# Layer 3 of a spectral network: where two pieces of statistics stand in the VectorE queue

## The chip, the cores and the metric

The kernel runs on one core of a Trainium2 chip. The metric is the device time of one execution in microseconds, lower is better; the time shown for a kernel is the median of its timed executions. Engines are called by the names of the profile: PE is TensorE (PEld its weight loads), DVE is VectorE, ACT is ScalarE, POOL is GpSimd, and SP is SyncE, which here only issues DMAs.

## The reference

Eight images of 8 channels and 256x256 pixels pass through two layers with residuals. The first normalizes x over groups and runs a small Fourier neural operator on it: a lift to 40 channels, four rounds of a spectral convolution (12x12 low and high modes) plus a grouped 1x1 convolution, with a gated activation after the first three, and then two 1x1 convolutions with 512 channels between them. The second normalizes again and takes a 3x3 maximum.

```python
def ref(xg):                                   # _L0_conv_ref, x normalized in groups
    h = gconv1x1(concat(xg, grid), fc0_w, fc0_b)
    for i in range(4):
        h1 = spectral_conv(h, sp_w1[i], sp_w2[i])
        h2 = gconv1x1(h, w_w[i], w_b[i])
        h = h1 + h2
        if i < 3:
            h = gswish(h, betas[i])
    h = gswish(gconv1x1(h, fc1_w, fc1_b), betas[3])
    return gconv1x1(h, fc2_w, fc2_b)
x = x + ref(gn(x))
x = x + dilate3x3(gn(x))
```

`gn` needs mean and variance of x over each of four groups of two channels, for each image. Everything is in float32.

## The kernel before

The images run one after the other, and the work of an image is laid over that of its neighbours. For image b, `layers` runs the four layers (`l` from 0 to 3). Each has a short spectral part (`spectrum_h`, `mix`: modes by weights, on DVE mostly), then the rows of the inverse transform (`rows_even` or `rows_odd`: matmuls into PSUM banks `p_g`, copied into the SBUF tile `zt`), and then `layer`: 11 chunks of pixels, for each a `burst(c)` of matmuls into `p_z`, first the 1x1 convolution (L590), then the columns of the inverse transform out of `zt` (L593), and an ACT instruction that writes h back (L598, or L600 in layer 3, after which L602 stores the chunk to DRAM).

Three other strands are woven in. The head of the image before (fc1, activation, fc2 and the sum into y) is cut into steps: `first` is four matmuls into `p_fc` (L813) and two ACT activations (L814, L815); `second` is fc2 (L830), whose sum DVE adds to y (L839). The tail of the image before is the dilation, on DVE (L877 to L893). The third strand is `side`, the generator `start(b + 1)`: the statistics and spectrum of the next image's x (`spectrum_x`). It advances by one piece for each `next(side, None)`. Its first two pieces are the two passes of the loop at L268: four `bn_stats` (L271) each, one per group, on one half of x in `turned`. What comes after is `bn_aggr` (L275), the sums over partitions on PE (L260, L262), the reciprocal root, the normalization (L296), and the transforms. For the last image there is no next one, and `side` yields nothing.

The order of instructions on PE, DVE, ACT and SP is the order in which the Python code emits them (`tc.manual_schedule`); semaphores are put in from the tiles that are read and written. The generators yield short strings that name what to weave in at that point: "f" is a `first`, "c" a `second`, "t" a piece of the tail. Image 0 has no head before it, so nothing is woven into its layers (`alone[0]`).

The lines that the change touches are in `rows_odd`, which serves layers 1 and 3. It makes the rows in two groups: (0..5) and (6..9). Each takes four PSUM banks, one from the ring "one" and three from the ring "tri", both of two buffers, which `p_fc` and `p_z` share. The matmuls of a group are at L509. `copy_banks` shares its copies out (L215 on ACT, L217 on DVE); in the second group ACT has copies 1, 4 and 5 and DVE has 0, 2 and 3. In layer 3 a piece of `side` is taken after each group: after the first group's copies and the head's steps "fc", and after the second group's copies and "f". `hold(last)` then ties loads that were held back behind the last row matmul.

The image 0..7 of this text is b of the code. The first burst of layer 3 needs the `zt` copies of both groups for L593, and a free `tri` buffer for L590.

Of the kernel before, what the change touches and what calls it, by code (L numbers as in the profile page):

```python
# [46 lines left out]
def fno_dilate_kernel(ctx: ExitStack, tc: tile.TileContext, a: dict, out: bass.AP):  # L47
# [17 lines left out]
    def ps_four(name):  # L65
        one, tri = ps_a(f"{name}_0"), ps_tri(f"{name}_1")
        return one, tri, [one] + [tri[:, i, :] for i in range(3)]

    def part(i):
        return slice(32 * i, 32 * i + 32)  # L70
# [139 lines left out]
    def copy_banks(pairs, by_act):  # L210

        done = []
        for i, (dst, src) in enumerate(pairs):
            if i in by_act:
                ins = nc.scalar.activation(dst, src, AF.Identity).ins  # L215
            else:
                ins = nc.vector.tensor_copy(dst, src).ins  # L217
            for other in done:
                if other.engine != ins.engine:
                    tc.declare_no_dep(ins, other, reason="two engines read banks of one tile and write apart")  # L220
            done.append(ins)
# [274 lines left out]
    def rows_odd(b, l, side):  # L496

        zv = zt[:, :, :, : NBLK * WID].rearrange("p r g (n o) -> p g o n r", n=NBLK)
        hold()
        yield "ffc"  # L500
        for part_of, by_act, kinds in ((((0, 1, 2), (3, 4, 5)), (2, 3), "fc"), (((9,), (6, 7, 8)), (1, 4, 5), "f")):
            one, tri, banks = ps_four(f"p_g_{b}_{l}_{part_of[0][0]}")
            pairs = []
            for i, os in enumerate(part_of):
                for at, o in enumerate(os):
                    for j in range(NQ):
                        for k in range(2):
                            two = slice(64 * k, 64 * k + 64)
                            last = mm(banks[2 * i + k][part(j), 2 * NBLK * CS * at : 2 * NBLK * CS * (at + 1)],  # L509
                                      fz2[two, o, :], rowg[two, j].rearrange("p g x -> p (g x)"),  # L510
                                      start=True, stop=True)
                for k in range(2):
                    src = banks[2 * i + k][:, : 2 * NBLK * CS * len(os)]
                    src = src.rearrange("p (o g n r) -> p g o n r", g=2, n=NBLK, r=CS)
                    dst = zv[:, 2 * k : 2 * k + 2, os[0] : os[-1] + 1]
                    if len(os) == 1:
                        pairs.append((dst[:, :, 0], src[:, :, 0]))
                    else:
                        pairs += [(dst[:, g], src[:, g]) for g in range(2)]
            copy_banks(pairs, by_act)  # L520
            yield kinds
            if l == 3:
                next(side, None)
        hold(last)
        if l < 3:
            yield "t"
# [164 lines left out]
    def layers(b, stored, d, then, ahead):  # L691

        for l in range(4):
            if l > 0:
                yield from spectrum_h(b, l, d)
                yield from mix(b, l, d)
            yield from rows_odd(b, l, then) if l % 2 else rows_even(b, l)  # L700
            yield from layer(b, l, d, stored, then, ahead)
        yield "stored"
        yield from rest(b, then)
# [60 lines left out]
    def hold(after=None):  # L764

        due, held[0] = held[0], [] if after is None else None
        for f in due or ():
            tc.add_manual_dep(f().ins, after.ins.name, BEHIND, reason="load behind the rows")
# [355 lines left out]
```

## Time and profile before

| what | value |
|---|---|
| three timed runs | 3701.52, 3705.54, 3706.05 us |
| median | 3705.54 us |
| profiled execution | 3705.41 us |
| its span, first to last instruction | 3703.6 us |
| mean granted PE clock | 0.977 |
| PE busy | 3495.7 us (94%) |
| ACT busy | 2864.6 us (77%) |
| DVE busy | 2385.4 us (64%) |
| `bn_stats` on x (L271) | 64 instructions, median 678 ns |
| `zt` copies on DVE (L217) | 266 instructions, median 533 ns |

The span is the time between the first and the last instruction of the profiled execution; the execution's own time is 1.8 us longer. Busy PE is not PE at its peak: matmuls are pipelined, and the ends of their records are modelled. Rows of the timeline give the start in us from the span's beginning, the length in us, engine, line, operation, output and inputs, shape, how many are merged into the row, and in brackets the idle time of the engine just before with what ended it. The releaser is inferred: of several that a wait asks for, the one that came last by the profile. The chain of waits goes back from the last instruction to what released it, step by step. In the table of windows the granted clock of PE stands after the five engines, as a share of full speed.

### The profile page before, as it was taken

The page shows a single profiled execution, that of the slowest core. Times are in us where ns is not written, and L with a number is a line of the kernel's source. Part 1 is how long each engine was busy: PE and PEld are TensorE (multiplying, and loading weights), DVE is VectorE, ACT ScalarE, POOL GpSimd, SP SyncE. Part 2 cuts the span into 40 slices and gives each one's busy share as a digit, 9 for nine tenths or more (in the row PEclk, how much of TensorE's full clock was granted, in tenths as well). Part 3 has the DMA queues.
Part 4 walks back from the last instruction along what each step waited for, and adds up shares of the span by engine and source line. Part 5 has one row for each costly group of instructions (what it writes and reads, how often), then busy time and mean ns, then how long its engine had stood idle before and what let it go on. Part 6 is the DMA issues. An engine that isn't in the chain of part 4 may idle for free.

```text
span 3703.6 us, 112658 instructions
## 1 busy us (share of the span) xinstructions
PE 3495.7 (94%) x50872; PEld 1271.0 (34%) x50872; DVE 2385.4 (64%) x3711; ACT 2864.6 (77%) x3021; POOL 117.1 (3%) x202
## 2 busy tenths in 40 slices
PE   5768999999999999999999999999999999999997
PEld 2323333333333333333333333333333333333222
DVE  6776666557775677746776577765777567772443
ACT  2435888888788888787887878888888878879986
POOL 1000000000000000000000000000000000000000
PEclk7878999999999999999999999999999999999998
DMA  3005111432225212261223512244222522225221
GB/s 91 16 19 205 52 50 46 160 110 72 72 83 190 81 55 66 92 220 52 60 62 125 181 55 74 65 159 122 64 75 89 183 76 61 72 64 194 82 83 48
DMA packets 114081, 344.71 MB, mean 93 GB/s; under 512 B 15985, under 2 KB 18481, under 8 KB 98177
## 3 DMA queue, kind: packets, MB, share of 16 engines
q1 hardware_dynamic: 95392, 276.32, 24.6%
q0 software_dynamic: 18208, 61.18, 5.0%
q8 instruction: 400, 6.55, 0.7%
q14 instruction: 81, 0.66, 0.1%
HBM read 213.44 MB, written 123.74 MB: 91 GB/s over the span
## 4 chain that ended last, share of the span: by engine, by line
PE 73%; DVE 16%; issue 4%; ACT 4%; DMA 2%; POOL 0%; ACTq 0%; DVEq 0%; POOLq 0%
PE p_fc L830 20%; PE p_fc L813 19%; PE p_z L593 9%; PE p_z L590 7%; PE p_d L558 7%; PE p_z L587 3%; DVE y L839 3%; PE p_u L572 3%; DVE turned L541 3%; DVE S L414 3%; DVE turned L411 2%; DMA yin<-y_rows 2%; PE p_b L381 1%; ACT act L815 1%; ACT act L814 1%
## 5 line engine op out<-in xcount | busy, mean ns | idle before, releaser
L815 ACT ACTIVATE act<-p_fc 128x1536 f32<-128x1536 f32 x1024 | 1493.1, 1458 | 0.0
L813 PE MATMUL p_fc<-hs,c_w 32*128 32x512 f32 x8192 | 1133.2, 625 | 40.2 <-DVE y L839 20.8
L830 PE MATMUL p_fc<-act,c_w 128*32 128x512 f32 x8192 | 1008.6, 601 | 0.2 <-ACT act L815 0.2
L814 ACT ACTIVATE act<-p_fc 128x512 f32<-128x512 f32 x1024 | 616.5, 602 | 229.7 <-PE p_fc L813 218.2
L541 DVE STREAM_TRANSPOSE turned<-h 128x1024 f32<-128x1024 f32 x528 | 632.7, 1226 | 189.7 <-ACT h L598 189.2
L598 ACT ACTIVATE h<-p_z 128x512 f32<-128x512 f32 (+1 forms) x528 | 511.9, 1021 | 212.2 <-PE p_z L593 212.2
L839 DVE TENSOR_TENSOR y<-p_fc,y 128x512 f32<-128x512 f32 x392 | 267.7, 683 | 553.9 <-PE p_fc L830 553.9
L813 PEld LDWEIGHTS p_fc<-hs,c_w 32*128 32x128 f32 x8192 | 357.7, 183 | 612.8 <-ACT act L814 253.3
L830 PEld LDWEIGHTS p_fc<-act,c_w 128*32 128x32 f32 x8192 | 221.8, 109 | 705.0 <-issue 330.7
L593 PE MATMUL p_z<-c_binv,zt 32*128 32x256 f32 x5632 | 411.7, 406 | 2.1 <-DVE zt L217 2.1
L590 PE MATMUL p_z<-h,c_wt 32*32 32x512 f32 x8448 | 363.5, 606 | 15.7 <-DVE zt L217 7.7
L593 PEld LDWEIGHTS p_z<-c_binv,zt 32*128 32x128 f32 x5632 | 259.8, 187 | 312.4 <-issue 300.0
L558 PE MATMUL p_d<-turned,c_fw 32*32 32x480 f32 (+1 forms) x9216 | 307.8, 539 | 0.6 <-DVE turned L541 0.2
L600 ACT ACTIVATE h<-p_z,c_bias 128x512 f32<-128x512 f32 (+1 forms) x176 | 186.4, 1110 | 89.1 <-PE p_z L593 89.0
L562 ACT ACTIVATE turned<-p_d 128x1440 f32<-128x1440 f32 x144 | 182.9, 1270 | 89.7 <-PE p_d L558 86.5
L215 ACT ACTIVATE zt<-p_g 128x198 f32<-128x198 f32 (+2 forms) x118 | 53.4, 575 | 182.8 <-PE p_g L487 99.9
L414 DVE TENSOR_REDUCE S<-turned 128x80 f32<-128x800 f32 x192 | 189.0, 984 | 5.9
L411 DVE TENSOR_TENSOR turned<-t,B 128x800 f32<-128x800 f32 x192 | 188.7, 983 | 0.9
L558 PEld LDWEIGHTS p_d<-turned,c_fw 32*32 32x32 f32 x9216 | 127.0, 103 | 165.8 <-issue 64.9
L372 DVE STREAM_TRANSPOSE turned<-zt 128x960 f32<-128x960 f32 x96 | 176.8, 1865 | 2.5
L590 PEld LDWEIGHTS p_z<-h,c_wt 32*32 32x32 f32 x8448 | 93.2, 103 | 186.8 <-DVE y L839 48.8
L572 PE MATMUL p_u<-turned,c_stack 128*32 128x480 f32 (+1 forms) x1152 | 136.7, 543 | 11.6 <-DVE turned L561 6.2
(192 smaller groups left out, 1762.8 us busy)
## 6 DMA issues: line engine op xcount, KB each, us to landing
stored<-h SPq DMA_DIRECT2D x88, 1024.0 KB
hs<-stored SPq DMA_DIRECT2D x352, 256.0 KB
t<-in_spw SPq DMA_DIRECT2D x96, 400.0 KB
yin<-y_rows POOLq DMA_DIRECT2D x56, 512.0 KB, 5.2
h<-in_xp SPq DMA_DIRECT2D x352, 48.0 KB
turned<-in_xw SPq DMA_DIRECT2D x16, 1024.0 KB
y<-in_x SPq DMA_DIRECT2D x56, 256.0 KB
y_rows<-y POOLq DMA_DIRECT2D x56, 256.0 KB, 3.9
```

What stands on the lines that cost most here:

```text
L411: nc.vector.tensor_tensor(pr, sw[k], bt[:, k2, k].unsqueeze(2).to_broadcast([128, G, 2 * WID, WID]), ALU.mult)
L414: nc.vector.tensor_reduce(s[k2][:, k].rearrange("p s o g -> p (s o) g"), pr.rearrange("p g m i -> p m g i"), AX.X, ALU.add,)
L541: nc.vector.transpose(dst[:, 2 * i : 2 * i + 2], h[:, c, 2 * i : 2 * i + 2].rearrange("p f (s x) -> p f s x", s=2))
L558: mm(banks[q][part(v % 4), : 240 * n], fw8[part(q), v, :], t[part(q), :, :, v, : NBLK * WID], start=v < 4, stop=v >= 4)
L590: mm(o, wt[part(q), l, g, :], h[part(q), c, f, :], start=True, stop=False)
L593: mm(banks[q][:, HW * s : HW * (s + 1)], zt[part(q), 2 * c + s].rearrange("p f o -> p (f o)"), binv[part(q), :], start=False, stop=s == 1)
L598: nc.scalar.activation(dst, src, AF.Silu)
L813: mm(banks[g], w1[part(g), blk, :], hs[k][part(g), :], start=True, stop=True)
L814: nc.scalar.activation(act[:, 0, :], one, AF.Silu)
L815: nc.scalar.activation(act[:, 1:4, :], tri, AF.Silu)
L830: mm(acc[part(g), :], w2[:, g, 15 - rb - i : 47 - rb - i], act[:, g, :], start=i == 0, stop=i == 1)
L839: nc.vector.tensor_tensor(y, sums, y, ALU.add)
```

## The change

In layer 3, `next(side, None)` is no longer called in the loop over the two row groups; it is called twice behind the loop, still ahead of `hold(last)`.

```diff
             copy_banks(pairs, by_act)
             yield kinds
-            if l == 3:
-                next(side, None)
+        for _ in range(2 if l == 3 else 0):
+            next(side, None)
         hold(last)
         if l < 3:
             yield "t"
```

On DVE, in images 0 to 6, the order was: copies of the first group, (addition L839), four `bn_stats`, three copies of the second group, four `bn_stats`. It becomes: copies of the first group, (addition L839), three copies of the second group, eight `bn_stats`. The addition is there in images 1 to 6. The orders on the other engines stay as they are, and so does what each instruction waits for. Layer 1, which runs the same function, doesn't change.

## The prediction

> **What bounds the kernel now.** I read the page first, then the chain of waits in the stretches where layer 3 begins, then the timeline of all engines in those stretches, and last the table of windows with the granted clock. From the page, the shares of the chain that ended last by engine:
>
> ```profile
> PE 73%; DVE 16%; issue 4%; ACT 4%; DMA 2%; POOL 0%; ACTq 0%; DVEq 0%; POOLq 0%
> ```
>
> So the end is set by TensorE (PE) for most of the span and by VectorE (DVE) for a sixth of it; a piece of DVE work that stands on the chain is worth its length. The statistics (L271) are such a piece. Chain of waits around the start of layer 3 of image 1 (start, us, what):
>
> ```profile
> 689.03 0.69 DVE y L839
> ...
> 690.24 1.86 DVE bn_x L271 x3
> 692.10 0.30 DVE zt L217
> ...
> 692.45 1.92 PE p_z L590 x32
> ```
>
> The chain leaves PE at 689.0, goes through an addition, through four `bn_stats`, through the first copy into `zt`, and comes back to PE at 692.45. The statistics belong to the next image, and nothing near here needs them: they are on the chain because DVE takes its queue in order and the copies stand behind them. The timeline of the same place, all engines:
>
> ```profile
> 689.64 2.46 DVE L271 BATCH_NORM_STATS2 bn_x<-turned 128x6 f32<-128x512 f32 x4
> 690.03 1.14 PE L813 MATMUL p_fc<-hs,c_w 32*128 32x512 f32 x8
> 690.13 1.09 ACT L215 ACTIVATE zt<-p_g 128x132 f32<-128x132 f32 x3 [1.01 <-PE p_g L509]
> 691.74 1.45 ACT L815 ACTIVATE act<-p_fc 128x1536 f32<-128x1536 f32 x1
> 692.02 1.06 DVE L217 COPY zt<-p_g 128x132 f32<-128x132 f32 x3
> 693.19 0.27 PEld L590 LDWEIGHTS p_z<-h,c_wt 32*32 32x32 f32 x30 [0.62 <-ACT act L815]
> 694.30 1.15 PE L593 MATMUL p_z<-c_binv,zt 32*128 32x256 f32 x16
> 695.46 2.12 ACT L600 ACTIVATE h<-p_z,c_bias 128x512 f32<-128x512 f32 x2 [2.28 <-PE p_z L593]
> ```
>
> ACT copies its three banks of the second row group at 690.13, as soon as PE has made them; DVE copies its three only at 692.02. PE ends `p_fc` at 691.17 and stands until 692.45, makes two pieces of L590, and stands again to 693.19, the end of the last DVE copy (692.02+1.06 = 693.08) plus 0.11. The row names ACT L815 for that second stop because it too ends at 693.19; but L815 reads the other `tri` buffer. `p_z` takes the buffer of `p_g`, two takings back in a ring of two, and waits for the `zt` copies. ACT then stands 2.28 us before L600. Both engines have run dry, and the work that would fill them waits for three copies.
>
> The kernel holds its own counter-sample. Image 7 has no next image, so no statistics stand there. The same stretch of image 7:
>
> ```profile
> 3332.28 1.36 DVE L217 COPY zt<-p_g 128x132 f32<-128x132 f32 x3
> 3332.67 1.14 PE L813 MATMUL p_fc<-hs,c_w 32*128 32x512 f32 x8
> 3332.77 1.11 ACT L215 ACTIVATE zt<-p_g 128x132 f32<-128x132 f32 x3 [1.01 <-PE p_g L509]
> 3333.74 1.35 PE L590 MATMUL p_z<-h,c_wt 32*32 32x512 f32 x32
> 3335.01 1.15 PE L593 MATMUL p_z<-c_binv,zt 32*128 32x256 f32 x16
> ```
>
> From the start of L813 to the start of L593 it is 2.34 us here, against 694.30-690.03 = 4.27 in image 1.
>
> [...] the bank was there by 690.13 (ACT took its share then) and DVE came 1.89 us later. [...] The trace shows such half-rate windows right behind this stall in images 0, 3 and 4; the windows of image 3, with busy times of PE, PEld, DVE, ACT, POOL, then the granted clock:
>
> ```profile
> 1568.30:1571.60 3.30, 2.02 (x26) 0.52 (x20) 3.30 (x8) 3.03 (x5) 0.00 (x0) 0.99 0.45 128
> 1571.70:1575.00 3.30, 3.30 (x47) 1.42 (x45) 1.99 (x4) 0.00 (x0) 0.00 (x0) 0.51 0.08 28
> ```
>
> PE was busy 2.02 of 3.30 us in the stretch with the stall, and the next ran at 0.51. Images 1, 2, 5 and 6 had the same stall and no such window[...]. [...]
>
> **The change part by part.** It removes and adds no instruction. On DVE, in images 0 to 6, four `bn_stats` (2.46 us) go from ahead of the three copies of the second row group to behind them, next to the other four. PE, ACT, POOL and SP keep their order, and every instruction waits for the same producers as before; no DMA moves in any queue. The two halves of x which the statistics read have landed already (DVE shows no idle time before them), and they are read later than now.
>
> *Images 1 to 6.* DVE ends the addition at 689.72 and turns to the copies; they end as in image 7, 3333.64-3331.53 = 2.11 us after the row matmuls (L509) began, so at 688.89+2.11 = 691.00 instead of 693.08. PE is busy with L813 to 691.17, ACT copies to 691.22: what is late next is those, not DVE. By image 7 the gain to L593 is 4.27-2.34 = 1.93 us per image; by the waits, 694.30 less (691.22+0.14+1.08, the L590 block after its last bank is free) = 1.86. I take 1.93, since it is measured with the copies of both engines side by side, and keep 1.86. Six images: 11.6 us. In the other five the row L590 shows 1.27 or 1.28 us of idle time, like image 1, so one number serves for all.
>
> Does it last? ACT, 2.28 us idle before L600, would be 0.35 us idle, as in image 7. From L593 of burst 0 to L590 of burst 1 it is 4.89 us in image 1 and 4.90 in image 7: the lead isn't lost on the way. Loads and stores are issued by these same instructions and move with them.
>
> *What stands behind the statistics now.* The eight in a row end about 690.9+4.85 = 695.75 (now 695.36). Behind them is the addition L839, whose matmul now ends at 698.15, then at 696.22: 0.5 us of room. The aggregation (L275) comes after that addition, and PE asks for it at 705.43. Cost: nothing, covered by that 0.5 us; if the cover were gone, each us more delays the bank that the next burst takes.
>
> *Image 0.* Nothing is interleaved here, and the path is another one:
>
> ```profile
> 296.70 2.42 DVE L271 BATCH_NORM_STATS2 bn_x<-turned 128x6 f32<-128x512 f32 x4
> 299.03 1.04 DVE L217 COPY zt<-p_g 128x132 f32<-128x132 f32 x3
> 300.22 1.15 PE L593 MATMUL p_z<-c_binv,zt 32*128 32x256 f32 x16 [2.10 <-DVE zt L217]
> 304.94 0.49 PE L260 MATMUL p_st_x<-mv_x,avg 128*128 128x4 f32 x2
> ```
>
> The copies would end at 296.70+1.04 = 297.74 and L593 follow L590 at once, at 298.05: 2.17 us earlier. But then L260 needs the statistics, which end when they do now, plus the same 0.14 or so: the aggregation at 302.85, L260 at 302.97 instead of 304.94. PE arrives at 301.4 and waits 1.6 us. So image 0 gains 304.94-302.97 = 1.97, and the releaser changes from the copies to the statistics. The bounds: 0.4 us, if that new wait trips a half-rate window (priced below at 1.55), and 2.17, if the statistics come sooner than thought. I take 1.97.
>
> *Half-rate windows.* In image 3, L590 takes 2.79 us against 1.92 in image 1 and L593 1.83 against 1.15: 0.87+0.68 = 1.55 us; image 4 is alike (2.79 and 1.89). With the stall gone PE is idle for a few tenths in such a stretch, and I take both windows as gone: 3.1 us (image 0's lies where PE will wait anyhow, and counts nothing). Bounds: nothing, if windows fall elsewhere instead (four more lie in other parts of the span), and some 5 us, if one or two of those go too.
>
> *Sum.* 11.6+1.97+3.1 = 16.7 us. The profiled execution took 3705.41 us, 3703.6 of them in the span; 3705.41-16.7 = 3688.7. The median of the runs shown, 3705.54, lies 0.1 above this execution, so it stands for them. I forecast 3689.
>
> **The rivals.**
> 1. The stall goes, the windows do not: the two of images 3 and 4 land elsewhere and image 0 makes one. 3705.4-11.6-0.4 = 3693.4. For it: [...] the runs before spread over 4.5 us. Against it: three of the seven stalls were followed by one at once, none after image 7's start without a stall.
> 2. ACT is the pace of layer 3, and a lead beyond its idle time is lost. Before L600 of burst 1 ACT is idle for only 0.47 us; if just that is kept, 6×0.47+2.0 = 4.8, so 3700.6. Against it: image 7, where the lead lasts into burst 1.
> 3. The change doesn't do what it says: L590 waits for ACT L815, as the row of 693.19 has it. Then only image 0 gains, 3703.4. Against it: image 7's L590 begins at 3333.74, before its L815 (3334.38); and in image 0 a row without an L815 has the same 0.11 us after a DVE copy.
> 4. Slower: the block of eight holds up the addition L839, its bank and so burst 1, and in image 0 the aggregation. It decides once the block ends more than 0.5+1.93 = 2.4 us later than worked out, that is at 0.92 us a piece instead of 0.61. At 1.0 us a piece: 3.1-2.43 = 0.7 lost in each of six images, and 1.1 in image 0: some 5 us, 3710.5. Against it: both groups of four run at 0.61 now, one beside matmuls and the other beside ACT.
>
> **How the numbers follow.** The forecast as it stands 0.62, rival 1 0.23, rival 2 0.07, rival 3 0.04, rival 4 0.04. The likeliest gives 3689. The range reaches from 3685 (gone windows elsewhere too) to 3697 (rival 1 with one or two windows more), which leaves rivals 2 to 4 out. Within 0.2% (7.4 us, about what a measurement can tell from no change) lie rivals 2 and 3; faster by more is anything below 3698.1: 0.86; same 0.10; slower 0.04.
>
> **What would show it.** Right: L271 is gone from the chain in images 1 to 6; L813 to L593 takes about 2.3 us in each; ACT is idle some 0.35 us before the first L600; L839 still waits for PE behind the block; in image 0, L260 waits for the aggregation; no half-rate window right behind the start of layer 3. Wrong: L590 still waiting at its old distance, L839 starting late behind L271, or a longer idle time later in layer 3 that takes the lead back.

## The result, and the profile after

| | before | changed |
|---|---|---|
| median of 6 timed runs | 3703.75 us (3700.28 to 3706.05) | 3689.73 us (3682.43 to 3695.7) |
| profiled execution | 3705.41 us | 3688.73 us |
| its span | 3703.6 us | 3687.0 us |

The ratio is 0.9962, with a 95% interval from 0.9951 to 0.9973. The two profiled executions lie 16.7 us apart, the medians 14.0.

The chain of waits at the start of layer 3 of image 1, in the changed kernel (start, length, what):

```profile
686.40 1.13 PE p_g L509 x63
687.53 1.07 PE p_fc L813 x8
688.60 1.27 PE p_z L590 x32
689.88 1.08 PE p_z L593 x16
```

Addition, statistics and copy are gone from it; PE goes from one block to the next. The timeline of all engines there:

```profile
687.07 1.36 DVE L217 COPY zt<-p_g 128x132 f32<-128x132 f32 x3
687.46 1.14 PE L813 MATMUL p_fc<-hs,c_w 32*128 32x512 f32 x8
687.57 1.11 ACT L215 ACTIVATE zt<-p_g 128x132 f32<-128x132 f32 x3 [1.01 <-PE p_g L509]
688.28 4.80 DVE L271 BATCH_NORM_STATS2 bn_x<-turned 128x6 f32<-128x512 f32 x8
688.53 1.35 PE L590 MATMUL p_z<-h,c_wt 32*32 32x512 f32 x32
689.81 1.15 PE L593 MATMUL p_z<-c_binv,zt 32*128 32x256 f32 x16
690.97 2.12 ACT L600 ACTIVATE h<-p_z,c_bias 128x512 f32<-128x512 f32 x2 [0.35 <-PE p_z L593]
693.73 0.69 DVE L839 TENSOR_TENSOR y<-p_fc,y 128x512 f32<-128x512 f32 x1 [0.65 <-PE p_fc L830]
```

From L813 to L593 it is 2.35 us, as it was in image 7 before; L590 has no idle time left in its row, ACT stands 0.35 us before L600 instead of 2.28, and the eight statistics run under all of this. The addition behind them still finds DVE idle, by 0.65 us.

In image 0 the chain passes through the statistics in another way:

```profile
295.96 1.63 DVE zt L217 x5
297.60 4.64 DVE bn_x L271 x8
302.24 0.34 DVE mv_x L275 x4
...
302.71 0.36 PE p_st_x L260 x2
```

The copies are done early, L593 starts at 297.86, and PE runs on until L260, which asks for the aggregation. The block of eight is the bound there now.

To see where the time went, each ACT instruction of the one profile can be set against the same instruction of the other, since their order is the same. The lead is the start in before less the start in the changed kernel, as the median over a dozen instructions on each side of a step; "between" is what happened from there to the next image.

```
start of layer 3    lead in -> out    gained   between
image 0             0.25 ->  2.60      2.35     -0.03
image 1             2.57 ->  4.49      1.92     +0.51
image 2             5.00 ->  6.83      1.83     -4.05   two half-rate windows more
image 3             2.78 ->  6.18      3.40     +3.18   two fewer
image 4             9.36 -> 13.01      3.65     +0.03
image 5            13.04 -> 14.96      1.92     -1.55   one more
image 6            13.41 -> 15.26      1.85     +1.42   one fewer
```

The seven starts give 16.9 us, and the last instruction leads by 16.7. What lies between adds up to -0.5 us, but only because half-rate windows came and went in equal number. By this table a window counts for 1.4 to 2.0 us.

### The profile page after: what moved, and what is told of

Read it like the earlier page. It is cut to its first block, busy times and chain, and to the rows that moved or that the text cites. A ratio compares the mean times of both kernels' runs of the same rounds, so it can differ in the third digit from the quotient of the medians.

```text
span 3687.0 us, 112658 instructions
## 1 busy us (share of the span) xinstructions
PE 3486.2 (95%) x50872; PEld 1270.1 (34%) x50872; DVE 2386.8 (65%) x3711; ACT 2865.0 (78%) x3021; POOL 117.1 (3%) x202
## 4 chain that ended last, share of the span: by engine, by line
PE 73%; DVE 16%; issue 5%; ACT 4%; DMA 2%; POOL 0%; ACTq 0%; DVEq 0%; POOLq 0%
PE p_fc L830 20%; PE p_fc L813 19%; PE p_z L593 9%; PE p_d L558 7%; PE p_z L590 7%; PE p_z L587 3%; DVE y L839 3%; PE p_u L572 3%; DVE turned L541 3%; DVE S L414 3%; DVE turned L411 2%; DMA yin<-y_rows 2%; DVE turned L372 1%; PE p_b L381 1%; PE p_g L509 1%
## 5 line engine op out<-in xcount | busy, mean ns | idle before, releaser
L815 ACT ACTIVATE act<-p_fc 128x1536 f32<-128x1536 f32 x1024 | 1493.2, 1458 | 0.0
L813 PE MATMUL p_fc<-hs,c_w 32*128 32x512 f32 x8192 | 1133.4, 625 | 41.2 <-DVE y L839 20.8
L839 DVE TENSOR_TENSOR y<-p_fc,y 128x512 f32<-128x512 f32 x392 | 267.9, 684 | 539.1 <-PE p_fc L830 539.1
L813 PEld LDWEIGHTS p_fc<-hs,c_w 32*128 32x128 f32 x8192 | 358.3, 183 | 613.4 <-ACT act L814 253.3
L593 PE MATMUL p_z<-c_binv,zt 32*128 32x256 f32 x5632 | 410.3, 405 | 0.0
L590 PE MATMUL p_z<-h,c_wt 32*32 32x512 f32 x8448 | 357.8, 601 | 7.9 <-ACT act L814 4.2
L593 PEld LDWEIGHTS p_z<-c_binv,zt 32*128 32x128 f32 x5632 | 258.9, 186 | 308.0 <-issue 295.1
L600 ACT ACTIVATE h<-p_z,c_bias 128x512 f32<-128x512 f32 (+1 forms) x176 | 186.4, 1110 | 72.0 <-PE p_z L593 71.8
L590 PEld LDWEIGHTS p_z<-h,c_wt 32*32 32x32 f32 x8448 | 92.9, 103 | 175.3 <-DVE y L839 48.8
```

Source lines behind the costliest of these rows:

```text
L590: mm(o, wt[part(q), l, g, :], h[part(q), c, f, :], start=True, stop=False)
L593: mm(banks[q][:, HW * s : HW * (s + 1)], zt[part(q), 2 * c + s].rearrange("p f o -> p (f o)"), binv[part(q), :], start=False, stop=s == 1)
L813: mm(banks[g], w1[part(g), blk, :], hs[k][part(g), :], start=True, stop=True)
L815: nc.scalar.activation(act[:, 1:4, :], tri, AF.Silu)
L839: nc.vector.tensor_tensor(y, sums, y, ALU.add)
```

## The experiments

The half-rate windows of PE after the first layers, from the clock record of each trace (start in us; 3.4 us long, or 6.8 where two follow each other, marked with x2; the granted clock in them is 0.50 in before and in the changed kernel). The stretch of 24 to 25 us at half rate at the very end, which every trace has, is left out. The kernels in the list are explained below.

```
before            302, 1572, 1653, 1677, 2015, 2974, 3548
changed           1206, 1230, 2544, 3531
changed, again    359, 1209, 1233, 1650, 2111 x2, 3537
image0_only       1648, 2089, 2969, 3543
images1to6_only   301, 772, 2523, 3533
both_ahead        301 x2, 700, 1140 x2, 1584 x2, 2028 x2, 2471 x2, 2915 x2, 3571
four_more_behind  794 x2, 1214, 1583, 2023, 2559, 2999
one_more_behind   768, 2519, 2959, 3533
image0_in_gap     1643, 2521, 3531
```

**Image 0 alone, and images 1 to 6 alone.** Two kernels make the change for one part of the images each.

```diff
-            if l == 3:
+            if l == 3 and not alone[0]:
                 next(side, None)
+        for _ in range(2 if l == 3 and alone[0] else 0):
+            next(side, None)
         hold(last)
```

> The statistics go behind the copies in image 0 only. Theory (each image pays its own stall, and a lead once won is kept): in the profile the layer-3 start of image 0 gains about 2.3 us over before (L260 released by the aggregation, near 302.7 us), and images 1 to 6 keep 4.27 us from the start of L813 to the start of L593. The time moves by 2.3 us at most, plus or minus some half-rate windows of 1.6 us. Rival (image 0's lead is swallowed by the DMA-heavy stretch behind it, 310 to 340 us): the lead is back to zero at 400 us.

One execution took 3700.88 us. The lead over before goes from 1.6 us ahead of the start of image 0 to 4.0 behind it, so 2.4 are won there, and it stands at 3.8 us at 545 us: the stretch full of DMAs (their share is 1.00 to 1.02 from 310 to 340 us in before) doesn't take it. Images 1 to 6 keep 4.27 us from L813 to L593. The same new wait is seen as in the changed kernel:

```profile
301.32 0.35 PE L260 MATMUL p_st_x<-mv_x,avg 128*128 128x4 f32 x2 [1.52 <-DVE mv_x L275]
```

The absolute place, 302.7, wasn't reached because this execution was 1.6 us ahead before anything had changed.

The other half has `not alone[0]` and `alone[0]` exchanged.

> The statistics go behind the copies in images 1 to 6 only; image 0 as before. Theory: 6 times 1.9 = 11.4 us less than before from the stalls, plus what half-rate windows behind them cost before (0 to 3 us): some 3690 to 3692 against a before of 3703.75. L813 to L593 is about 2.35 us in images 1 to 6, and image 0 keeps its half-rate window near 302 us. Rival (most of the gain was image 0 and luck with the half-rate windows): 3698 or more.

3690.61 us, ratio 0.9958 (0.9943 to 0.9973). The distance is 2.35 or 2.36 us in all six images, and image 0 keeps its window, at 301. The gain is images 1 to 6 for the most part.

**Both pieces ahead of the copies.** The stall is made longer, to see whether the price follows the length and whether the half-rate windows follow the stall.

```diff
-            if l == 3:
+            for _ in range(2 if l == 3 and part_of[0][0] == 0 else 0):
                 next(side, None)
```

> Both pieces stand ahead of the second group's copies, so that eight bn_stats precede them. Theory: each of the seven stalls grows by 2.44 us, so 6 times 2.44 = 14.6 us more than before in images 1 to 6 and up to 2.4 in image 0; [...] a half-rate window follows nearly every stall (5 more at 1.5 us, 7.5): 3718 to 3728 against 3703.75. L813 to L593 is 6.7 us or more. Rival A (ACT sets the pace of layer 3 and takes up a delay of PE): under 3712. Rival B (half-rate windows fall by chance and not behind stalls): 3718 to 3721 and no more such windows at the seven places than in the profile of before.

3728.31 us, ratio 1.0063 (1.0048 to 1.0078). That is 0.3 us above the upper end of what the theory gave (3718 to 3728), and past both rivals. TensorE in image 3, as a timeline and then in three windows (busy PE, PEld, DVE, ACT, POOL, then the granted clock):

```profile
1579.88 1.14 PE L813 MATMUL p_fc<-hs,c_w 32*128 32x512 f32 x8
1581.75 1.04 PE L590 MATMUL p_z<-h,c_wt 32*32 32x512 f32 x2 [0.73 <-ACT act L814]
1585.42 2.02 PE L590 MATMUL p_z<-h,c_wt 32*32 32x512 f32 x30 [2.63 <-DVE zt L217]
1587.37 2.09 PE L593 MATMUL p_z<-c_binv,zt 32*128 32x256 f32 x16
```

```profile
1581.00:1584.20 3.20, 1.06 (x6) 0.13 (x2) 3.20 (x6) 2.01 (x3) 0.00 (x0) 0.97 0.53 161
1584.30:1587.60 3.30, 2.18 (x34) 0.54 (x38) 0.98 (x4) 0.00 (x0) 0.00 (x0) 0.50 0.00 0
1587.70:1591.00 3.30, 3.30 (x26) 1.60 (x22) 0.00 (x0) 1.52 (x2) 0.00 (x0) 0.53 0.00 0
```

From L813 to L593 it is now 7.49 us in images 2 to 6 and 6.65 in image 1. Behind the stop, 30 pieces of L590 take 2.02 us (all 32 took 1.35 in image 7 of before), and L593 takes 2.09 instead of 1.15. That nearly every stall would be followed by a half-rate window was an estimate; all seven starts are followed by one, six of them by two (in image 3 the two rows above at 0.50 and 0.53). Here the second stop of L590 has the right name: the wait for the copy ends long after ACT L815.

**More work behind the eight.** Rival 4 rested on the room that the addition L839 has. In images 1 to 6, further `bn_stats`, whose result is not used, follow the eight: one or four.

```diff
         for _ in range(2 if l == 3 else 0):
             next(side, None)
+        if l == 3 and not alone[0] and b + 1 < n_img:
+            more = sb.tile([128, 6], F32, tag="bn_more", bufs=1, name=f"bn_more{b}")
+            for i in range(4):
+                nc.vector.bn_stats(more, turned[:, 1, 512 * i : 512 * i + 512])
         hold(last)
```

> As the change, with one more bn_stats (0.61 us) in images 1 to 6 behind the eight; its result is not used. Theory (the block has 0.65 us of room before the addition L839 is asked for): no cost or a tenth of a us per image. From L593 of burst 0 to L590 of burst 1 it stays at 4.89 us, and the time is that of the changed kernel within its spread, 3686 to 3693. Rival (every us behind the copies costs, room or not): 6 times 0.6 = 3.6 us more, and 5.3 us or more between those two points.

3689.69 us, ratio 0.9957 (0.994 to 0.9973). DVE in image 1 (the addition is L843 here, since lines moved by four):

```profile
686.21 1.36 DVE L217 COPY zt<-p_g 128x132 f32<-128x132 f32 x3
687.41 4.80 DVE L271 BATCH_NORM_STATS2 bn_x<-turned 128x6 f32<-128x512 f32 x8
692.14 0.67 DVE L527 BATCH_NORM_STATS2 bn_more<-turned 128x6 f32<-128x512 f32 x1
692.87 0.69 DVE L843 TENSOR_TENSOR y<-p_fc,y 128x512 f32<-128x512 f32 x1
```

The addition comes 7.27 us after the one before it, as in the changed kernel (693.73 against 686.46), and bursts 0 and 1 stay 4.89 us apart in all six images. The room is used up and nothing is lost.

> As the change, with four more bn_stats in images 1 to 6 behind the eight; their result is not used. Theory (the addition L839 stands behind the block with about 0.6 us of room, and PE needs its bank almost at once): the block ends 2.4 to 2.8 us later, the addition comes 1.8 to 2.2 us late, and burst 1 starts 1.6 to 2.1 us late in each of six images: 10 to 13 us more than the changed kernel, 3700 to 3703, that is all of the gain in images 1 to 6. Rival (nothing waits for that addition soon, ACT is the pace there): 3689 to 3692, with the addition late in the profile and the first L590 of burst 1 not.

3705.39 us, ratio 1.0004 (0.9995 to 1.0013): all that the change had won is gone, and a little more than expected. The chain in image 1:

```profile
690.10 4.65 DVE bn_x L271 x8
694.75 0.60 DVE bn_more L527
...
696.84 0.69 DVE bn_more L527
697.53 0.60 DVE y L843
...
698.18 1.15 PE p_z L594 x32
```

Statistics, addition, first matmuls of burst 1, with nothing between: the block is on the chain again, now by way of the addition. From L593 to burst 1's L590 (L597 and L594 in this kernel) it is 6.70 us instead of 4.89, so 1.81 are lost in each image, within the 1.6 to 2.1 that were expected. The time lies above the expected 3700 to 3703. The profiled execution has three half-rate windows more than the changed kernel's first (seven against four), two of them behind the new stall at burst 1 (1583 and 2023). At 1.6 us each they make 4.8 us, and with 6 times 1.81 that is 15.7 us, the distance of the medians (3705.39-3689.73). That fits, but the windows of the other executions aren't known.

**Image 0: half of the statistics into a gap of DVE.** The new wait in image 0 can be taken away too. The four of the first piece go ahead of the first group's copies, where DVE waits for row matmuls.

```diff
         hold()
         yield "ffc"
+        if l == 3 and alone[0]:
+            next(side, None)
...
-        for _ in range(2 if l == 3 else 0):
+        for _ in range((1 if alone[0] else 2) if l == 3 else 0):
             next(side, None)
```

> As the change in images 1 to 6; in image 0 the first four bn_stats go further ahead, in front of the first group's copies, where DVE waits for row matmuls. Theory: DVE's waiting time there (1.80 and 0.46 us before the copies) covers all but some 0.15 us of the 2.45, the aggregation ends near 300.5 us instead of 302.6, and the wait of L260 for it (1.52 us in the changed kernel) goes: the lead over before behind image 0 is 3.7 to 4.0 us instead of 2.6, with 3686 to 3690 as time, which the spread hides. Rival (the first group's copies come late by the length of the block): L590 of burst 0 starts over 0.5 us late in its second part and the lead is under 2.6.

3688.61 us, ratio 0.9957 (0.9944 to 0.9969). In the timeline of image 0:

```profile
292.05 2.46 DVE L271 BATCH_NORM_STATS2 bn_x<-turned 128x6 f32<-128x512 f32 x4
294.43 3.53 DVE L217 COPY zt<-p_g 128x198 f32<-128x198 f32 x9
297.77 2.46 DVE L271 BATCH_NORM_STATS2 bn_x<-turned 128x6 f32<-128x512 f32 x4
301.40 0.39 PE L260 MATMUL p_st_x<-mv_x,avg 128*128 128x4 f32 x2
```

L260 no longer waits. Counted from the copy L465 ahead of it all (291.63 here, 291.38 in the changed kernel), L260 comes after 9.77 us instead of 11.33. The lead behind image 0 is 3.54 us, short of the 3.7 expected; it had none before, where the changed kernel's 2.60 began with 0.25, so some 1.2 us are won against the changed kernel. The medians, 3688.61 and 3690.85 on the same chip, are too close for their spread to tell this apart. Its profiled execution, 3688.35 us, is the shortest of those profiled, but only by 0.4 us, and with one half-rate window less than the changed kernel's first (three against four); so no run here shows that this order is faster as a whole.

**The changed kernel once more.**

> The changed kernel once more, unaltered. Theory: the profile has no half-rate window within 7 us behind the start of layer 3 in any image, while such windows lie elsewhere in number and place not as in its first profile; each costs about 1.6 us, so the time of the execution differs from 3688.7 by some 1.6 us for each window more or less. Rival (the windows stand at fixed places in the program): the same four, near 1206, 1230, 2544 and 3531 us.

3690.85 us, ratio 0.9966 (0.9955 to 0.9977). Its profiled execution took 3694.95 us, 6.2 more than the first one. It has seven half-rate windows instead of four: three more, 4.8 us by the price of 1.6; most of the remaining 1.4 is a start-up that was 1.2 us slower. None of them stands behind a start of layer 3. The rival is partly right, though: windows near 1206, 1230 and 3531 us are there again. More than that, in all nine traces the windows that follow no start of layer 3 stand at few places of the program: 77 to 79 or 100 to 102 us behind the first L600 of one of the images 1 to 6, or 211 to 213 us behind that of image 7. Outside these are only 359 here and the two behind the new stall of four_more_behind. Which of the places get a window differs from trace to trace.

At the first place PE had just stopped (1.81 us at 1203 in the changed kernel); at the second it had not. The stretch ahead of the window at 1230 and the window itself, with the same columns as in the windows of both_ahead:

```profile
1226.58:1229.99 3.41, 3.41 (x83) 1.37 (x80) 0.17 (x1) 2.88 (x6) 0.00 (x0) 1.00 0.02 5
1229.99:1233.40 3.41, 3.41 (x40) 1.92 (x24) 2.10 (x2) 1.92 (x3) 0.00 (x0) 0.50 0.00 0
```

PE was busy throughout by its records, and the clock dropped all the same: a stall isn't the only thing that a half-rate window can follow.

## Why the prediction was right

- *What bounds.* Right. The chain lost its DVE detour in images 1 to 6 and went to PE, as the experiment with both pieces ahead and the one with four more behind show from both sides.
- *1.93 us per image, taken from image 7.* Measured 1.92, 1.83, 1.92 and 1.85 in the images without a half-rate window. From L813 to L593 it is 2.35 against the 2.34 of image 7. The second way to the number, by the last wait, gave 1.86. The lead is not lost on the way (rival 2): from L593 to burst 1 it is 4.89 us before and after the change wherever no half-rate window lies in between, and in the experiments too, unless so much was added that the addition came late.
- *What stands behind the statistics.* Nothing, as predicted; the room was 0.65 us, not 0.5. Its edge was found: one more `bn_stats` is free, four more cost 1.81 us per image. Rival 4 was a real mechanism that had not been reached.
- *Image 0.* The new wait came where it was put, L260 on the aggregation, at 302.71. Less the 0.25 us that the start-up gave, that is 1.98 us won, against 1.97. But the image gained 2.35: the working ended at L260 and left out that what stands behind it could move by another amount. The L590 of burst 2 came 0.83 us behind L260 before (305.77-304.94) and comes 0.46 behind it now (303.17-302.71). Its row in before, in the changed kernel and in the one with the statistics in the gap (L592 there):

```profile
305.77 1.15 PE L590 MATMUL p_z<-h,c_wt 32*32 32x512 f32 x32 [0.17 <-ACT h L600]
303.17 1.16 PE L590 MATMUL p_z<-h,c_wt 32*32 32x512 f32 x32
302.23 1.15 PE L592 MATMUL p_z<-h,c_wt 32*32 32x512 f32 x32 [0.27 <-ACT h L602]
```

Before, it waited for ACT's copy of burst 1; now ACT copies while PE waits for the aggregation. The half-rate window of before, which "counts nothing", reached to 305.2 and had its part (L593 of burst 1 took 2.09 us, L260 to L262 0.42 against 0.29), but the 0.83 doesn't need it: with the statistics in the gap there is no such window, and the distance is 0.83 us again (302.23-301.40), with the wait for ACT.
- *Half-rate windows.* Both of images 3 and 4 went, 3.40 and 3.65 us instead of 1.9, so 3.2 us against 3.1. That they stood behind the stall is shown: 7 of 7 starts with the doubled stall have one, 4 of 14 with the stall of before (3 of 7 in before, none of 6 in the kernel with image 0 alone, image 0 in its counterpart), none of 35 without the stall. Rival 1 failed for these windows; elsewhere in the span three came and three went, and 1206 and 1230, which came, stand at the same two places of the program as 1653 and 1677, which went, but in image 2 and not in image 3.
- *The sum.* 16.7 us were worked out, and 16.7 separate the two profiled executions. That it agrees to a tenth is luck in part: image 0 gave 0.4 more than its term and the start-up 0.25, and some 0.5 were lost between the images. That the medians are 14.0 apart, and 3689 nonetheless near 3689.73, is luck in part too: the profiled execution of before stood 1.7 us above the later median of before, and that of the changed kernel 1.0 below its own.

Left open: why the clock drops at one of these places in one image and not in the next. The windows were counted in the profiled executions only, but the mean granted clock is on record for every one, and most of the spread goes with it: of the 29 executions of before that ran beside the experiments, the five at 0.979 took 3699.65 to 3702.57 us, and the seven at 0.975 or 0.976 took 3707.92 to 3714.28.

## What to carry to other kernels

Work that nobody near needs, queued on DVE ahead of copies that free PSUM banks, held them up here: DVE came to the copies 1.89 us after ACT had begun on the same group of banks. With nothing else for PE and ACT to do, that cost most of the work's length (in image 1, 1.93 us for the 2.46 of the first four `bn_stats`, and 2.38 more for four more ahead of the copies). Behind the copies the work was free up to the idle time in front of the next instruction that somebody needs (0.65 us: one more `bn_stats` cost nothing, four more 1.81 us per image). Look for a place in the same trace where the suspected work is missing (here the last image): the difference of the two distances is the price, with all overlaps in it. Where an engine waits for several buffers, ask whose buffer it takes before believing the named releaser.

## What the runs showed of the hardware

A stall of PE can cost more than its length: its clock was granted at half rate (0.50) for 3.4 us, or twice that, behind some stalls, and each such window cost about 1.6 us of span here (images 3 and 4 of before took 1.57 and 1.62 us longer from L813 to burst 1 than the other images with the same stop). A stop of 1.28 us in a row of busy work, with a short second one behind it (0.62 us of PEld in image 1), was followed by one in 2 of 12 cases (images 1 to 6); stops of 2.10 and 1.90 us in 2 of 2 (image 0); 1.74 us ahead of burst 1 in 2 of 6; 3.4 us of stops (0.73 and 2.63) in all of six; the new wait of L260 in image 0, 1.45 to 1.64 us, in none of five.

In the traces of before and of the changed kernel (its first profile), all changes of the granted clock lie whole multiples of 3.4133 us apart, to 0.01 us; the starts listed above for the other seven traces fit that spacing to the full us in which they are given. In the 3.41 us ahead of a listed half-rate window of these two, PE was busy for 1.27 to 2.13 us, or, at 1230, 1677 and 2544, for all of it. Of the six short stops of before, four (images 1, 3, 4 and 6) fell whole into one stretch between two such multiples. PE was busy for 2.13 of its 3.41 us in all four, and two of them (images 3 and 4) were followed by half rate. So neither the length of the stop nor the busy time of its stretch decided here, and what did was not shown. The two profiles of the changed kernel differ by three half-rate windows and by 6.2 us.
